# Two cross-attention layers on one core: the zeros of layer 0's transposed contexts set on GpSimd when their buffers are handed out

## The chip, the core and the metric

The kernel runs on one core of one Trainium2 chip. Its time is the device time of one execution in microseconds (us). The profile is one further execution, taken by the hardware profiler. Engines: PE (TensorE's matmuls; PEld its weight loads), DVE (VectorE), ACT (ScalarE), POOL (GpSimd), and SP (SyncE), which here only issues transfers; "SPq" rows are those issues. Every engine works through its own list of instructions in order; an instruction that waits holds up all behind it on that engine. SyncE's list is in order too: a transfer whose source or destination is not ready holds up the issue of all later ones.

## The reference

All data is float32. `x` is 8 batches of 100 rows of 512, `ctx_2048` 8 batches of 361 rows of 512.

```python
# layer 0, one head of 512
q = x @ w_q.T;  k = ctx @ w_k.T;  v = ctx @ w_v.T
probs = softmax(q @ k.T / sqrt(512))
x = x + alpha * ((probs @ v) @ w_o.T)
# layer 1: twice (1, 2) a cross-attention with 16 heads of 128, then an MLP
h = layer_norm(x)
kh = concat(ctx @ wk + bk, bias_k);  vh = concat(ctx @ wv + bv, bias_v)   # 361 + 1 keys
x = x + softmax((h @ wq + bq) @ kh.T / sqrt(128)) @ vh @ wo + bo
x = x + gelu(layer_norm(x) @ w_fc1 + b_fc1) @ w_fc2 + b_fc2
```

## The kernel before

Weights are multiplied together where that saves work: layer 0 needs only `wqk` and `wvo`, and in the layers after it the queries are multiplied with `wk` ("wide queries", `pqw`, L687), so that scores are taken against the raw context. For that every batch's context is needed transposed.

**The transposed contexts.** `ctx_transposed(b)` (L450) makes a tile `cT` of 128 partitions x 7 blocks x 2 x 181 numbers. The 361 keys are split in 181 and 180, so the second half has one padded key; the four blocks B11, B21, B22, T3 are what layer 0's scores read, T1, T2 and T4 are sums that later layers use. TensorE transposes (`pcT`, L457), ScalarE copies into B21, B22 and B11 (L460, L461, L463), VectorE subtracts into T3 (L464) and makes T2, T1, T4 (L466 to L468), which read whole blocks with the padded key. So the padded column must be zero: L452 sets it on VectorE, as the first instruction of the function. At the end the tile is stored to DRAM (`cTd`, L469, 1267 KB), from where the later layers load it again (L182).

**The ring.** `cT` tiles have two slots (`C_SLOTS`). A `Ring` (L23) keeps the planned order of uses; `issue()` makes a tile as soon as the ring's next slot is free of planned uses, and calls its `fill`:

```python
            key = self.order[self.next]
            name = "_".join(map(str, key))
            self.tiles[key] = self.pool.tile(self.shape, F32, tag=self.tag, name=name)
            self.fill(key, self.tiles[key])
```

For a later layer's `cT`, `fill_cT` (L180) issues the load from DRAM. For layer 0's (key[1] is -1) it does nothing, since the tile is written by compute. The pool gives out its slots in the order in which a scheduler meets the first instruction on each tile; what waits for the slot is that first instruction, and every other engine that writes the tile waits for the slot's last users as well.

**The order of layer 0** is written in `layer0_units` (L527). For each batch b: `l0_probs(b)` (transposes of the weights, `ppt` L348), `l0_scores(b + 1)` (`sc` L478, then L331 on VectorE and the exponential L334 on ScalarE), `l0_mixed(b)` (`pxc` L511, copied by ScalarE L514), `ctx_sums(b)`, `ctx_transposed(b + 2)`, the scaling (L341, L342) of b + 1, loads of the weights `wqe` (L156 on GpSimd's queue), `l0_out(b)` (`pd` L520, L521), which also stores the rows of x (`xd`, L376). `ctx_sums(b)` (L437) makes five sums of context blocks on GpSimd (L441 to L445) in one buffer (`msum`, bufs=1) and stores them to DRAM (`cxd`, L447, L448); the next batch's sums wait until both stores have landed. VectorE also multiplies the `wqe` weights (`bias_sums`, L603). In what follows, "cT 7" is layer 0's transposed context of batch 7.

**SyncE's queue** mixes all of this: at the end of layer 0 it issues, in this order, the store of cT 6 (L469), rows of x, a weight load, the load of layer 1's first cT (L182), the stores of batch 5's sums (L447, L448), the store of cT 7, rows of x, the stores of batch 6's sums with loads of layer 1's second context between them (L169 to L178, and a second L182), rows of x, a weight load, the stores of batch 7's sums, rows of x, then the bias scores of layer 1 (`sbd`, L647) and their return as one number per partition (`nsb`, L652, L653), and the weights of the heads, a pair at a time (`wkr`, `wq`, L156; `wkd`, L663).

**Layer 1's start.** `normed` (L566) takes the rows of x, `project_units` (L1132) makes transposed weights (`pwk`, L661), queries (`pq`, L671) and wide queries for two heads at a time. The first scores (`sc`, L478) go through L331, L334, L341 and L342 and are transposed on VectorE (L358). For the second block of queries the rows of x are loaded again (`xr`, L370) and normalised on VectorE (L579).

Of the kernel before, what the change touches and what calls it, by code (L numbers as in the profile page):

```python
# [38 lines left out]
KH = 181  # L39
B11, B21, B22, T1, T2, T3, T4 = range(7)  # L40
# [39 lines left out]
def two_cross_attentions(ctx: ExitStack, tc: tile.TileContext, a: dict, out: bass.AP):  # L80
    nc = tc.nc
# [10 lines left out]
    def psum(pool, shape, name):  # L92
        return pool.tile(shape, F32, tag=pool.name, name=name)
# [84 lines left out]
        nc.sync.dma_start(out=t[:TS, :, A33, :], in_=d[:TS, :, 0, :])  # L178

    def fill_cT(key, t):  # L180
        if key[1] >= 0:
            nc.sync.dma_start(out=t.rearrange("p u c s -> p (u c s)"), in_=cTd[key[2]])  # L182

    rings = {
        "ctx": Ring(cpool, [P, 20 * P], "ctx", C_SLOTS, fill_ctx),
        "ctx0": Ring(work, [P, 9 * GWIDTH // 2], "pT", 2, fill_ctx0),
        "cT": Ring(cpool, [P, 7, 2, KH], "cT", C_SLOTS, fill_cT),
        "w": Ring(wpool, [P, 1024], "w", W_SLOTS, fill_w),
        "v": Ring(vpool, [P, 1024], "v", V_SLOTS, fill_w),
# [243 lines left out]
    def ctx0(b):  # L433
        t = rings["ctx0" if b % 2 else "ctx"].tiles["ctx", -1, b]
        return t[:, : 3 * D].rearrange("p (k n) -> p k n", k=3)
# [13 lines left out]

    def ctx_transposed(b):  # L450
        ct, cx = rings["cT"].tiles["cT", -1, b], ctx0(b)
        tc.keep_in_program_order(nc.vector.memset(ct[:, B22 : T3 + 1 : T3 - B22, :, KH - 1 :], 0.0))  # L452
        for c in (2, 3, 0, 1):
            ps = psum(ps_mm, [P, S], f"pcT_{b}_{c}")
            for t in range(3):
                w = TS if t == 2 else P
                nc.tensor.transpose(ps[:, t * P : t * P + w], cx[:w, t, c * P : (c + 1) * P], ident[:w, :w])  # L457
            left, right, n = ps[:, :KH], ps[:, KH:], S - KH
            if c >= 2:
                nc.scalar.copy(ct[:, B21, c - 2, :], left)  # L460
                nc.scalar.copy(ct[:, B22, c - 2, :n], right)  # L461
            else:
                nc.scalar.copy(ct[:, B11, c, :], left)  # L463
                nc.vector.tensor_tensor(ct[:, T3, c, :n], right, ct[:, B22, c, :n], ALU.subtract)  # L464

        nc.vector.tensor_tensor(ct[:, T2], ct[:, B11], ct[:, T3], ALU.subtract)  # L466
        nc.vector.tensor_tensor(ct[:, T1], ct[:, B22], ct[:, T2], ALU.subtract)
        nc.vector.tensor_tensor(ct[:, T4], ct[:, B21], ct[:, T2], ALU.subtract)  # L468
        nc.sync.dma_start(out=cTd[b], in_=ct.rearrange("p u c s -> p (u c s)"))  # L469
# [57 lines left out]
    def layer0_units():  # L527
# [3 lines left out]
        def turned(b):  # L531
            return [unit(lambda: ctx_transposed(b), key0("ctx", b), key0("cT", b))] if b < B else []
# [844 lines left out]
```

## Time and profile before

| | us |
|---|---|
| runs (3) | 2013.85, 2010.42, 2009.63 |
| median | 2010.42 |
| the profiled execution | 2009.43 |
| its span, first to last instruction | 2007.7 |
| mean granted TensorE clock in it | 0.998 |
| PE, PEld busy | 1959.0, 1811.7 |
| DVE, ACT, POOL busy | 1277.3, 757.0, 707.6 |

The groups of the page that belong to the change, and the waits from 120 to 182 us in which the stretch after it shows:

```profile
engine line waited for: us in total, times, longest us
POOL rstd L382 <- DVE var L381: 16.8, 3, 9.2
...
ACT cT_-1_7_955 L460 <- DMA cTd<-cT_-1_6_853: 7.0, 1, 7.0
POOL p L325 <- DMA nsb<-sbd: 6.9, 1, 6.9
...
PE sc L478 <- ACT cT_-1_7_955 L463: 4.1, 1, 4.1
...
DVE xr L579 <- DMA xr<-xd: 1.5, 1, 1.5
```

Each row names the engine and line that stood still, what released it, the total, the number of times and the longest. A name such as `cT_-1_7_955` is ring key (layer -1, batch 7) and a buffer number. The eight L452 memsets take 62 ns each; they start at 48.1, 67.3, 72.1, 82.2, 96.9, 107.1, 115.0 and 133.0 us. In the chain of waits, the profile follows the end of the execution back, from each instruction to what released it; a share in it is time on the path that sets the end. The windows give, for stretches of the span, the busy time of each engine, the granted TensorE clock (1.00 is full) and the transfers.

### The profile page before, as it was taken

To read this page: it belongs to the slowest core of one execution; us is meant where nothing else is said; L and a number is where in the kernel's file an instruction comes from. 1 tells how busy PE (TensorE), PEld (TensorE's weight loads), DVE (VectorE), ACT (ScalarE), POOL (GpSimd) and SP (SyncE) were. 2 spreads that over 40 slices of the span, in tenths; PEclk is the share of its full clock that TensorE was granted. 3 is DMA by queue.
4 is the path that set the end of the run, shared out by engine and by line. 5 is a ranking of instruction groups with operands and counts; after the bars stand their busy time and mean duration, and the time that the engine had idled before them with its cause. 6 is when DMAs were issued, how large, how long until landed. Compare 5 with 4: busy or idle time off the path is not lost.

```text
span 2007.7 us, 31493 instructions
## 1 busy us (share of the span) xinstructions
PE 1959.0 (98%) x10991; PEld 1811.7 (90%) x10991; DVE 1277.3 (64%) x3523; ACT 757.0 (38%) x2002; POOL 707.6 (35%) x1147
## 2 busy tenths in 40 slices
PE   9989999999999999999999999999999999999999
PEld 5678899998999899999999999999999999889998
DVE  2554776667677677666775766676666667765543
ACT  1324544344442343344432444444433444421231
POOL 3233432543344144525243323333243243325140
PEclk9999999999999999999999999999999999999999
DMA  7686224742645356625534453235234432136442
GB/s 253 247 310 217 93 76 138 225 136 68 195 146 166 107 142 204 200 71 164 181 120 127 116 182 103 85 92 164 88 117 130 135 123 83 58 86 190 119 127 73
DMA packets 250682, 283.89 MB, mean 141 GB/s; under 512 B 37608, under 2 KB 212108, under 8 KB 247196
## 3 DMA queue, kind: packets, MB, share of 16 engines
q1 hardware_dynamic: 246340, 271.51, 43.4%
q0 software_dynamic: 2112, 6.40, 0.9%
q10 hardware_dynamic: 2072, 3.97, 0.6%
q8 instruction: 88, 1.44, 0.3%
q14 instruction: 70, 0.57, 0.1%
HBM read 242.86 MB, written 38.97 MB: 140 GB/s over the span
## 4 chain that ended last, share of the span: by engine, by line
PE 78%; DVE 12%; ACT 4%; DMA 2%; issue 2%; POOL 1%; SPq 0%; DVEq 0%; ACTq 0%; POOLq 0%
PE sx L731 9%; PE mx L841 9%; PE mz L841 7%; PE pq L671 7%; PE po L891 7%; PE pqw L687 7%; PE pwo_P L954 7%; DVE pT L358 6%; PE sz L731 5%; PE my L841 3%; PE sy L731 2%; PE pfx L1094 2%; PE sc L478 2%; PE pgx L1045 2%; ACT p L342 1%
## 5 line engine op out<-in xcount | busy, mean ns | idle before, releaser
L358 DVE STREAM_TRANSPOSE pT<-p 32x192 f32<-32x192 f32 (+1 forms) x1664 | 602.2, 362 | 84.2 <-ACT p L342 53.0
L841 PE MATMUL mx<-pT,ctx 128*128 128x256 f32 (+3 forms) x960 | 280.3, 391 | 9.6 <-DVE Z L867 4.0
L731 PE MATMUL sx<-cT,Z 128*128 128x181 f32 x1152 | 228.2, 317 | 2.2 <-DVE p L771 2.2
L841 PE MATMUL mz<-pT,ctx 105*128 105x256 f32 (+3 forms) x768 | 207.2, 391 | 9.4 <-POOL pT L805 6.6
L765 POOL TENSOR_SCALAR p<-nsb 128x1 f32<-128x1 f32 x192 | 38.9, 222 | 492.0 <-DVE pT L358 452.9
L731 PEld LDWEIGHTS sx<-cT,Z 128*128 128x128 f32 x1152 | 194.5, 190 | 14.7 <-DVE p L771 3.7
L841 PEld LDWEIGHTS mx<-pT,ctx 128*128 128x128 f32 (+1 forms) x960 | 169.8, 189 | 29.0 <-DVE Z L867 7.1
L687 PE MATMUL pqw<-q,wkT 128*128 128x200 f32 x1024 | 194.4, 332 | 0.0
L891 PE MATMUL po<-Z,wv 128*128 128x200 f32 x1024 | 192.7, 332 | 0.0
L671 PE MATMUL pq<-hT,wq 128*128 128x200 f32 x1024 | 192.3, 332 | 0.0
L785 ACT ACTIVATE p<-p,nm 128x362 f32<-128x362 f32 x192 | 114.8, 598 | 187.1 <-DVE nm L784 184.7
L841 PEld LDWEIGHTS mz<-pT,ctx 128*128 128x128 f32 (+1 forms) x768 | 143.7, 190 | 42.7 <-POOL pT L805 9.2
L687 PEld LDWEIGHTS pqw<-q,wkT 128*128 128x128 f32 x1024 | 176.2, 189 | 4.8
L891 PEld LDWEIGHTS po<-Z,wv 128*128 128x128 f32 x1024 | 175.2, 189 | 3.4
L671 PEld LDWEIGHTS pq<-hT,wq 128*128 128x128 f32 x1024 | 175.3, 189 | 3.0
L784 DVE TENSOR_REDUCE nm<-p 128x1 f32<-128x362 f32 x192 | 101.6, 529 | 104.1 <-ACT p L776 94.0
L690 ACT COPY Z<-pqw 128x400 f32<-128x400 f32 x256 | 123.0, 490 | 78.3 <-PE pqw L687 78.3
L731 PE MATMUL sz<-cT,sums 128*128 128x181 f32 x768 | 149.3, 316 | 0.7 <-ACT p L759 0.7
L714 POOL TENSOR_TENSOR sums<-Z 128x256 f32<-128x256 f32 x96 | 70.7, 736 | 223.4 <-ACT Z L690 134.8
L342 ACT ACTIVATE p<-p,rden 128x362 f32<-128x362 f32 (+2 forms) x216 | 129.1, 599 | 28.0 <-DVE rden L341 28.0
L731 PEld LDWEIGHTS sz<-cT,sums 128*128 128x128 f32 x768 | 124.8, 189 | 1.0 <-ACT p L759 1.0
L841 PE MATMUL my<-pT,ctx 128*128 128x256 f32 (+3 forms) x384 | 102.5, 388 | 0.0
(380 smaller groups left out, 3125.0 us busy)
## 6 DMA issues: line engine op xcount, KB each, us to landing
wv<-in_L_xattn_wv_dram SPq DMA_DIRECT2D x64, 512.0 KB
wq<-in_L_xattn_wq_dram SPq DMA_DIRECT2D x64, 512.0 KB
wkT<-wkd SPq DMA_DIRECT2D x48, 512.0 KB
cT<-cTd SPq DMA_DIRECT2D x16, 1267.0 KB
wo_S<-wod SPq DMA_DIRECT2D x32, 512.0 KB
f<-in_L_xattn_w_fc_dram SPq DMA_DIRECT2D x32, 512.0 KB
wo_A<-in_L_xattn_wo_dram SPq DMA_DIRECT2D x24, 512.0 KB
xr<-xd SPq DMA_DIRECT2D x45, 200.0 KB
```

The costliest lines, as they stand in the source:

```text
L342: nc.scalar.mul(p[:rows, :n], p[:rows, :n], rden[:rows])
L358: nc.vector.transpose(dst[keys, :, :, i, :], src[i * QD : (i + 1) * QD, :, :, quarter, :])
L671: nc.tensor.matmul(ps, w[:, c, (h % 2) * K : (h % 2 + 1) * K], hTs[l, q][:, c, :], start=(c == 0), stop=(c == DT - 1),)
L687: nc.tensor.matmul(ps[:, c, :], w[:, h % 2, cc * P : (cc + 1) * P], qs[h], start=True, stop=True)
L690: nc.scalar.copy(Z[:, 2 * c2 : 2 * c2 + 2, :, h * L : (h + 1) * L], ps.rearrange("p c (b t) -> p c b t", b=QB),)
L714: nc.gpsimd.tensor_tensor(t[:, 0], a2[:, :2, :], a2[:, 2:, :], ALU.add)
L731: nc.tensor.matmul(ps[:, :KH], st["a"][a][:, c, :], st["ct"][:, blk, c, :], start=(first and c == 0), stop=(c == 1), skip_group_check=not ...
L784: nc.vector.tensor_reduce(nm, p[:, :S1], AX.X, ALU.max, negate=True)
L785: nc.scalar.activation(p[:, :S1], p[:, :S1], AF.Exp, bias=nm, accum_out=den)
L841: nc.tensor.matmul(ps, cx[:w, blk, :], pT[:w, u, :], start=first, stop=last, skip_group_check=more)
L891: nc.tensor.matmul(ps, w[:, c, (h % 2) * K : (h % 2 + 1) * K], Z[:, c, :, h * L : (h + 1) * L], start=(c == 0), stop=(c == DT - 1),)
L954: nc.tensor.matmul(ps, w[:, h, :], OB[i, j][:, h, :], start=(h == 0 and not more), stop=(h == 7), skip_group_check=more)
```

## The change

The memset of the padded keys leaves `ctx_transposed`, where VectorE ran it in a fixed place of its order, and goes into `fill_cT`, on GpSimd, with no fixed place. `fill_cT` runs when the ring hands the tile out, which for batch b + 2 is right after the scores of batch b. So the tile's first instruction comes earlier in the program and is another engine's.

```diff
     def fill_cT(key, t):
-        if key[1] >= 0:
+        if key[1] < 0:
+
+            nc.gpsimd.memset(t[:, B22 : T3 + 1 : T3 - B22, :, KH - 1 :], 0.0)
+        else:
             nc.sync.dma_start(out=t.rearrange("p u c s -> p (u c s)"), in_=cTd[key[2]])
...
     def ctx_transposed(b):
         ct, cx = rings["cT"].tiles["cT", -1, b], ctx0(b)
-        tc.keep_in_program_order(nc.vector.memset(ct[:, B22 : T3 + 1 : T3 - B22, :, KH - 1 :], 0.0))
         for c in (2, 3, 0, 1):
```

What it does to the order of the built program, by comparing the two builds engine by engine:

- VectorE: eight memsets less. At the end of layer 0 the steps L464 to L468 of cT 7 now stand ahead of L521 of batch 5, the copy L319 and the statistics. At layer 1's start both L579 of `xr` now stand ahead of the first L331; before, one stood behind it and the other some ten instructions further on.
- GpSimd: eight memsets more. Those of batches 0 and 1 come right after the start's own; the one of batch b + 2 stands ahead of the sums of batch b, or right behind them for b = 0. The five loads of `wqe` 0 to 4, which stood ahead of or right behind the sums of batch 0, now stand behind the memset of cT 2.
- ScalarE: the exponential of batch 7 ahead of the copy L514 of batch 6, and one pair of copies at layer 1's start exchanged.
- TensorE: one of the transposes L423 moved behind scores of batch 0. SyncE: one `wkr` load ahead of a `wkd` store.
- Waits: the first write of cT 7 waited for the store of cT 6; now it waits for the store of cT 5. The load of layer 1's first cT (L182) had no wait for a cT store of its own; now it waits for the store of cT 6.

## The prediction

> **What bounds the kernel now.** I read the page's shares first, then the chain of waits in order of time, then the windows and the SyncE queue around the place that the change touches. The page's part 4 says where the end comes from:
>
> ```profile
> PE 78%; DVE 12%; ACT 4%; DMA 2%; issue 2%; POOL 1%; SPq 0%; DVEq 0%; ACTq 0%; POOLq 0%
> ```
>
> The kernel is TensorE's; only 2% of the chain are transfers. The change touches layer 0 alone, the first 155 of 2008 us, so it can only be worth what stands in that stretch. The chain in order of time has two transfers there:
>
> ```profile
> 123.67 0.47 DVE p L331 x2
> 124.16 0.55 ACT p L334
> 124.70 8.28 DMA cTd<-cT_-1_6_853
> 133.06 0.31 ACT cT_-1_7_955 L460
> ...
> 134.28 5.15 PE sc L478 x16
> 139.43 3.08 PE pxc L511 x24
> ...
> 171.00 1.37 PE pq L671 x8
> 172.55 1.19 SPq L156
> 173.79 7.15 DMA xr<-xd
> 181.15 0.34 issue
> 181.68 0.61 ACT p L342
> ```
>
> First: batch 7's transposed context cannot be written until batch 6's has been stored, 8.28 us after SyncE issued the store. Second: x rows fetched again for layer 1's second query block (xr). After it the chain runs over VectorE (normalise xr, L341, transposes L358) up to 208 us and only then back to TensorE. The windows (length, PE, PEld, DVE, ACT, POOL, granted clock, DMA share, GB/s) show what the first costs:
>
> ```profile
> 130.00:132.00 2.00, 0.22 (x3) 0.03 (x1) 0.00 (x0) 0.00 (x0) 0.00 (x0) 1.00 0.91 297
> 132.00:134.00 2.00, 0.00 (x0) 0.00 (x0) 0.98 (x3) 0.94 (x5) 0.00 (x0) 0.83 1.11 437
> 134.00:136.00 2.00, 1.72 (x6) 1.66 (x7) 1.88 (x7) 0.44 (x3) 0.00 (x0) 0.50 0.94 381
> 136.00:138.00 2.00, 2.00 (x8) 1.93 (x7) 2.00 (x14) 0.00 (x0) 0.55 (x1) 0.50 0.80 302
> 138.00:140.00 2.00, 2.00 (x9) 1.95 (x9) 1.20 (x10) 0.00 (x0) 0.54 (x1) 0.50 0.98 409
> ```
>
> TensorE stands still for 4.1 us and then runs at half clock for 6 us.
>
> **What the change removes there.** With two slots, batch 7 should follow batch 5. In the build before, the layer 1 load of cT (L182) took batch 5's slot, and batch 7 waits for batch 6's store. The listing of both builds with their waits shows the swap: in the changed build the L460 copy of batch 7 waits for the store of batch 5, and the L182 load for the store of batch 6. Batch 5's store was issued at 110.93 and the DMA share had fallen to 0.32 by 119 to 120, so it has landed. The copy can start when ACT is free, at 126.05 instead of 133.06, and the scores follow batch 6's transposes at 130.2 instead of 134.28. Locally: 4.1 us of wait; scores 5.15 against 2.46 us for every other batch, 2.7; mix 3.08 against 2.65, 0.4. Sum **7.2 us** by which TensorE ends layer 0 earlier.
>
> **Small parts.** Eight VectorE memsets of 0.062 us go, 0.5 us at most. Eight GpSimd memsets come: the nearest rows are 0.12 us for 128x1 and three of 128x46 in 0.29 us, so 0.1 us each. Each stands ahead of L441's sums of a later batch, which wait for the cxd store anyway (35.7 us in six waits). Memset b+2 waits for the store of cT b, which SyncE issues before that cxd store. Nothing, therefore; if that cover went, 0.1 us each. The memset of batch 2 also stands ahead of five weight loads (wqe, L156), which move from 18.9 to 26.1 to about 55, when batch 0's store (issued at 50.27, moved by 54) is in. DMA moves nothing from 54 to 65, the loads landed 6.0 to 14.6 us after issue, and L603 needs the first at 91: nothing. Freeing the queues around 20 us gives nothing either, since TensorE waits for no load between 4.4 and 65 us.
>
> **What it moves, and what is late next.** The wait does not vanish: L182 now has it, in the middle of SyncE's queue.
>
> ```profile
> 124.70 0.34 SPq L469 DMA_DIRECT2D cTd<-cT_-1_6_853  x1
> 125.17 0.31 SPq L376 DMA_DIRECT2D xd<-O  x1
> 125.58 0.65 SPq L156 DMA_DIRECT2D wkr<-in_L_xattn_wk_dram  x1
> 126.29 1.59 SPq L182 DMA_DIRECT2D cT<-cTd  x1
> 127.97 2.08 SPq L447 DMA_DIRECT2D cxd<-msum  x1
> ...
> 144.01 0.55 SPq L182 DMA_DIRECT2D cT<-cTd  x1
> 144.61 0.59 SPq L447 DMA_DIRECT2D cxd<-msum  x1
> ```
>
> Behind it are the cxd stores of batch 5, the store of cT 7, and all that follows. GpSimd's sums of batch 6 need those cxd stores (there is one buffer) and began at 139.46; then the cxd stores of batch 6, sums of batch 7 (152.19), cxd stores of batch 7 (155.67), then the bias scores (159.24), their return (nsb), and at 164.26 the weights wkr of the third pair of heads. This chain of stores and sums never saw TensorE's wait, so TensorE's 7.2 us do not shorten it. How it shifts:
> - The store of cT 6 lands at 133.0 with the L182 load beside it. Alone, the same 1267 KB of batch 0 were moved 3.7 us after issue, which here is 128.4. I take 131: the ctx loads issued up to 124.2 are still ahead of it, but no load is beside it.
> - From the L182 load to the landing of the cxd stores behind it: the second pair above took 144.01 to 152.19, 8.2 us, with little ahead. So 131.1 + 8.2 = 139.3 against 139.46: **-0.2 us** (ends: -2.8 from 128.4, +1.8 from 133.0).
> - The bias scores no longer wait 1.3 us for VectorE's sT, but share the queue with the cxd stores of batch 7: I take 0.8 (ends 0 and 1.3).
> So wkr, and the 4.2 MB of weights from there to xr that keep the DMA at 0.84 to 1.10 from 166 to 180 us, come **1.0 us** earlier (ends: 4.1 earlier, 1.8 later). TensorE, 7.2 us early, reaches the third pair's transposes (L661) at 162.8 instead of 169.96 and waits: with wkr issued near 163.3 and, as before, at most 5.7 us to landing, until about 168.5. The gain is spent there, and xr lands at 180.0 instead of 181.03.
>
> Then VectorE's order counts. Before, the first layer 1 score (L331) ran at 178.91, ahead of xr's normalisation (L579, 181.03), and L341 followed at 181.49. In the changed build both L579 of xr stand ahead of L331. So after xr: two L579 (0.46 + 0.45, the second row set landing some 0.2 later), then L331 and the exponential, 1.6 us from L331 to L341's earliest start in the rows (0.53, 0.6, 0.19 and gaps): L341 at 180.0 + 2.5 = 182.5, 1.0 later. At 185.02 the second L579 is no longer in the way, -0.5. **Sum: +0.5 us** (ends -2.6 and +3.3) on a path that the chain shows to be the last up to 208 us. From there all engines' orders are the same, and the shift is carried to the end.
>
> TensorE's idle stretch of about 5.7 us will cost it its clock again. Rows: after 4.1 us of idle it had half clock from 134.3 to about 140.2; at the start 0.85 us instead of 0.43 a matmul up to 10.4. Six us at half clock cost 3 us; the first scores of layer 1 then end at 178.7 - 1.5 + 3.0 = 180.2, and L331 cannot start before 181.0 anyway: hidden, with 0.8 us to spare.
>
> The Trainium skill, TensorE: Matmul & The Clock Gate (Part 1), puts the half-rate stretch at about 3.4 us of sustained work, which would make that price 1.7 us; this trace has 6 us, and the trace decides. The Trainium skill, DMA: Bandwidth & Descriptors (Anatomy of one DMA), fits 2.0 us + bytes / 436e3; for 1267 KB that is an estimate of 5.0 us, a landing at 129.7 and a sum of -0.8 instead of +0.5; the 8.28 us of the trace, in a full queue, speak against it.
>
> **Rivals.**
> 1. The gain survives: 7.2 us less, 2002.7. For it: the two transfers on the chain are apart by 40 us, TensorE is 98% busy, and what TensorE has gained it would keep if xr came with it. Against: the cxd chain above, whose next start (139.46) stands on a DMA, not on TensorE. It would need the third pair's weights some 6 us earlier; no row moves them by more than 4.1.
> 2. Slower: the wait that L182 takes over. Everything behind it in SyncE's queue starts when the store of cT 6 lands, and the net is +0.5 at a landing of 131 with 0.8 from the bias scores. If those give nothing and it lands at 135, the net is 4.0 + 1.3 = +5.3, 2015.2. It exceeds 4 us from a landing of 133.7, just past the 133.0 of now; L182 alone is not on the queue to delay it, which speaks against.
> 3. It does not do what it says: batch 7 still waits, because its memset stands in GpSimd's queue behind other waits. Then the time stays as it is. Against: GpSimd is free at 119.6, 6 us ahead of the copy.
>
> **How the numbers follow.** The profiled execution took 2009.43 us (span 2007.7 and 1.7 around it); the median of the runs, 2010.42, lies 1.0 above it, the lowest 0.2 above. 2009.43 + 0.5, and 0.5 for a median's usual place: **2010.4**. About 0.2%, 4 us, is what a measurement of this kernel can tell from no change. Chances: the forecast 0.74, rival 3 with the same time 0.06, rival 1 (wholly or by over 4 us) 0.11, rival 2 0.09. So faster 0.11, same 0.80, slower 0.09. The range goes from 2009.43 - 2.6 to 2009.43 + 3.3 + 1.0, rounded outwards: 2006.5 to 2014.0.
>
> **What would show it.** Right: scores of batch 7 at about 130 us at full clock with no wait for a cT store; L182 on SyncE waiting until about 131; cxd of batch 7 still issued at about 155 to 156; a TensorE wait of 4 us or more for wkr near 163 with the clock low after it; xr landing near 180 and both L579 ahead of L331. Wrong: sums of batch 6 well before 137, no wait at the third pair's transposes, or xr landing before 177; then rival 1 wins. A landing of cT 6 after 133.7 makes it rival 2.

## The result, and the profile after

The changed kernel takes 2016.93 us (median of 8 runs, 2015.07 to 2020.16), the kernel before 2010.92 us (median of 8 runs): a ratio of 1.003, 95% interval 1.002 to 1.004. So it is about 6 us slower, and the interval lies clear of 1. The forecast was 2010.4 us with a range of 2006.5 to 2014.0, and "within 0.2%" at 0.80. It was wrong, on the side of rival 2.

The profiled execution took 2016.93 us, its span 2014.7. Below, lines up to 454 of the kernel before are +3 in the changed kernel and later ones +2. First the shares of the chain of waits after the change:

```profile
PE 78%; DVE 10%; DMA 4%; ACT 4%; issue 2%; POOL 1%; SPq 0%; DVEq 0%; ACTq 0%; POOLq 0%
```

Transfers have gone from 2% to 4%, VectorE from 12% to 10%. The wait that left ScalarE is now SyncE's, between 110 and 180 us, with a second one further on that comes up below:

```profile
SPq L156 <- DMA wkd<-wkT: 8.0, 2, 5.2
SPq L185 <- DMA cTd<-cT_-1_6_854: 6.8, 1, 6.8
```

(engine and line, what released it; us in total, times, longest). The chain in order of time (start us, length us, what) shows which transfers:

```profile
123.56 8.43 DMA cTd<-cT_-1_6_854
132.06 0.34 SPq L185
132.50 0.58 SPq L450
133.14 7.48 DMA cxd<-msum
140.78 0.73 POOL msum L444
...
146.06 7.41 DMA cxd<-msum
153.59 0.73 POOL msum L444
...
159.33 2.90 DMA sbd<-sT
162.24 0.55 SPq L654
...
164.91 0.65 SPq L156
165.61 6.67 DMA wq<-in_L_xattn_wq_dram
172.41 5.67 PE pq L673 x16
178.08 2.94 PE pqw L689 x16
181.03 2.46 PE sc L480 x16
```

Before, the chain left the store of cT 6 for TensorE's scores of batch 7. Now those scores run at 129.2 at full clock, and the chain stays with the transfers: store of cT 6, the load L185 that waits for it in SyncE's queue, cxd stores of batch 5, sums of batch 6, cxd stores of batch 6, sums of batch 7, bias scores (sbd, nsb), weights. TensorE, 8 us earlier than before at 154, stands still for the weights:

```profile
PE pwk L663 <- DMA wkr<-in_L_xattn_wk_dram: 4.1, 1, 4.1
PE pq L673 <- DMA wq<-in_L_xattn_wq_dram: 4.0, 2, 2.3
```

(in the same form). The first 2.3 us of the second row are the second pair's `wq`, before 159.06. What follows these waits, in windows (PE busy is the second number; the granted clock is the third from the right):

```profile
164.00:166.00 2.00, 0.74 (x5) 0.43 (x3) 0.00 (x0) 0.99 (x2) 0.31 (x2) 1.00 0.53 4
166.00:168.00 2.00, 0.00 (x0) 0.00 (x0) 0.00 (x0) 0.00 (x0) 2.00 (x8) 1.00 1.09 237
168.00:170.00 2.00, 1.21 (x6) 1.21 (x7) 0.00 (x0) 0.00 (x0) 2.00 (x4) 0.55 0.82 153
170.00:172.00 2.00, 0.76 (x4) 0.36 (x2) 0.69 (x1) 0.59 (x1) 0.08 (x1) 0.50 1.03 391
...
176.00:178.00 2.00, 2.00 (x8) 2.00 (x7) 0.00 (x0) 0.00 (x0) 0.00 (x0) 0.50 0.92 329
178.00:180.00 2.00, 2.00 (x12) 2.00 (x11) 0.00 (x0) 1.22 (x3) 0.00 (x0) 0.89 0.96 350
```

TensorE is at half clock from 168.2 to 178.4. It reaches layer 1's first scores at 180.9; before, at 176.25. VectorE is no earlier:

```profile
182.44 0.55 DVE L581 TENSOR_SCALAR xr<-xr,mv,rstd 100x512 f32<-100x512 f32 x1 [11.75 <-DMA xr<-xd]
183.40 0.55 DVE L581 TENSOR_SCALAR xr<-xr,mv,rstd 100x512 f32<-100x512 f32 x1 [0.41 <-DMA xr<-xd]
183.86 0.58 DVE L334 TENSOR_SCALAR_CACHE_REDUCE p<-sc,nsb 64x361 f32<-64x361 f32 x1
```

Both paths end within 0.4 us: the scores at 183.49, the second normalisation of `xr` at 183.86, when the row maximum (L334) starts. To see where the time goes in every run, I matched TensorE's instructions of each trace with those of before and noted how many us later (+) each comes, at five places of before's time:

| kernel | 60 | 154 | 173.5 | 195 | 300 | median - before |
|---|---|---|---|---|---|---|
| changed | -1.1 | -8.0 | +4.3 | +3.7 | +3.7 | +6.0 |
| e1 | -0.2 | +0.8 | +0.8 | +3.4 | +3.4 | +3.3 |
| e2 | -0.4 | -7.0 | +1.3 | +2.3 | +2.3 | +3.2 |
| e3 | 0.0 | -3.3 | -2.8 | -1.2 | -1.2 | +0.5 |
| e4 | +0.1 | +0.1 | +0.1 | +0.7 | +0.7 | +1.9 |
| e5 | -0.8 | -0.6 | -0.6 | -1.3 | -1.3 | +0.4 |
| e6 | -1.0 | -7.1 | -0.7 | -1.4 | -1.4 | +1.4 |
| e7 | -1.0 | -4.4 | +3.2 | +4.3 | +4.3 | +7.0 |
| e8 | -0.7 | -4.0 | +3.6 | +9.4 | +9.4 | +10.9 |
| e9 | +0.1 | -6.8 | -6.8 | -2.7 | -2.7 | +1.4 |
| e10 | +0.5 | -2.4 | -2.4 | -1.5 | -1.5 | -1.9 |
| e11 | -0.1 | -7.9 | -7.9 | -3.9 | -3.9 | -3.9 |
| e12 | -0.7 | -6.6 | -5.8 | -6.5 | -6.5 | -4.7 |
| e13 | -1.3 | -9.1 | -9.1 | -10.0 | -8.6 | -6.1 |
| e14 | -0.4 | -4.2 | +3.2 | +2.4 | +3.8 | +6.8 |
| e15 | 0.0 | -3.4 | +0.4 | -0.5 | +1.0 | +4.8 |
| e16 | -0.5 | -7.3 | -7.3 | -8.2 | -6.6 | -4.0 |

The first column is the start's scatter, not the change. The loss of the changed kernel lies between 154 and 195 us. From 300 us to the end every run loses 0.5 to 4.5 us more against before's profile, e3 too (3.6), whose order there is before's; I take the changed kernel's 3.3 there to be of that kind: before's one profiled execution, 1.5 us below its median, would then be a lucky one in that part. So the two traces place 3.7 us in this stretch; where the rest of the 6 us by the medians arises they do not settle. The medians decide.

**The gain in layer 0 differs from execution to execution.** The changed kernel, e6, e7, e8, e14 and e15 have one and the same order of every engine in layer 0, yet TensorE ends layer 0 at 146.5, 147.4, 150.1, 150.5, 150.3 and 151.2 us. Before's profile has 154.5; e3 and e10, whose tiles are claimed in before's order, have 151.2 and 152.2, and TensorE does not wait for batch 7's context in either. In e3:

```profile
114.54 0.81 DVE L603 SCALAR_TENSOR_TENSOR wqe<-wqe,Z 128x128 f32<-128x128 f32 x1
117.69 3.68 PE L520 MATMUL pd<-Z,xc 128*100 128x512 f32 x8 [1.43 <-ACT xc L514]
129.80 3.68 PE L520 MATMUL pd<-Z,xc 128*100 128x512 f32 x8 [1.81 <-ACT xc L514]
133.58 2.30 PE L478 MATMUL sc<-cT_-1_7_955,Z 128*100 128x181 f32 x12
```

VectorE's sums of `wqe` ran beside GpSimd's sums there (0.81 us instead of 0.28 for one; more on this with e1), TensorE waited 3.2 us for xc in two waits, and by then the store of cT 6 had almost landed: ScalarE's copy waited 0.9 us for it. In before's profile the two engines just missed each other, by 0.7 us at batch 4 (VectorE ends at 114.6, GpSimd begins at 115.31) and by 0.2 us at batch 5 (123.66, 123.88). So the wait of 4.1 us and the half clock behind it are those of an execution in which they miss. Where they meet, layer 0 ends at 150.1 to 151.2 with the early claim and at 151.2 and 152.2 without: some 1 us.

### The profile page after: what moved, and what is told of

Read it like the earlier page. It is cut to its first block, busy times and chain, and to the rows that moved or that the text cites. A ratio compares the mean times of both kernels' runs of the same rounds, so it can differ in the third digit from the quotient of the medians.

```text
span 2014.7 us, 31524 instructions
## 1 busy us (share of the span) xinstructions
PE 1961.0 (97%) x10991; PEld 1813.5 (90%) x10991; DVE 1280.3 (64%) x3515; ACT 756.6 (38%) x2002; POOL 708.5 (35%) x1155
## 4 chain that ended last, share of the span: by engine, by line
PE 78%; DVE 10%; DMA 4%; ACT 4%; issue 2%; POOL 1%; SPq 0%; DVEq 0%; ACTq 0%; POOLq 0%
PE sx L733 10%; PE mx L843 9%; PE mz L843 7%; PE pq L673 7%; PE pwo_P L956 7%; PE po L893 7%; PE pqw L689 7%; DVE pT L361 5%; PE sz L733 5%; PE my L843 3%; PE sy L733 2%; PE pfx L1096 2%; PE sc L480 2%; PE pgx L1047 2%; ACT p L345 1%
```

## The experiments

Theory A at the start: the wait that has moved into SyncE's queue delays all that stands behind it. Rivals: B, the transfers and the half clock take any gain of TensorE there; C, the zeros on GpSimd, or the weight loads held behind them, cost it.

**e1 and e2: the load out of the queue's way.** Same edit on the changed kernel (e1) and on the kernel before (e2).

```diff
+        elif key[1:] in ((0, 0), (0, 1)):
+            kept_cT[key[2]] = t            # loaded later by late_cT(b)
...
             res.append(unit(lambda b=b: ctx_sums(b), key0("ctx", b)))
+            if b >= 6:
+                res.append(unit(lambda b=b: late_cT(b - 6)))
```

> The changed kernel, with the first two layer 1 loads of cT issued later: that of batch 0 behind the cxd stores of batch 6, that of batch 1 behind those of batch 7, so that no load that waits for a store of a transposed context stands ahead of cxd stores in SyncE's queue. Theory A (the wait that moved into SyncE's queue delays the cxd stores, the sums, the bias scores and so the weights of the third pair): cxd of batch 5 issued near 127 instead of 132.5, third pair's wkr before 159 instead of 164.9, no TensorE wait over 1.5 us between 155 and 180, and the 5 to 7 us that TensorE gained at batch 7 stay: 2003 (2001 to 2006). Theory B (what TensorE gains is lost to the weights or to the half clock whatever SyncE's queue does): 2009 or more. Theory C (the zeros on GpSimd or the four weight loads held behind them are the loss): as the changed kernel, 2015 to 2018.

> The kernel before, with the same two loads issued later and nothing else: the zeros stay on VectorE, at the place where they were. With the load of batch 0 out of the way, batch 7's transposed context is the first to claim batch 5's place, as in the changed kernel. Theory A: the order of claims is all that the change brings, so the time is that of e1 within 2 us, 2003 (2001 to 2006). Theory C (GpSimd's part costs something): e1 is slower than this one by over 2 us. Theory B: 2009 or more in both.

Measured: e1 2014.26 us, 1.002 (1.0008 to 1.0032) of before; e2 2014.15, 1.002 (1.001 to 1.003). The two are equal, and 2.7 us below the changed kernel by the medians, but not at 2003: A alone doesn't hold. That they are equal speaks against C only weakly, since the traces show two different losses. In e2 TensorE keeps its 7 us up to 154, and then the chain reads

```profile
144.04 3.68 PE pd L527 x8
...
152.27 8.05 DMA sbd<-sT
160.34 0.55 SPq L661
...
163.01 0.66 SPq L156
163.72 6.65 DMA wq<-in_L_xattn_wq_dram
```

The bias scores go to memory at 152.27, 7 us earlier than in the changed kernel, but land after 8.05 us instead of 2.90, since my deferred 1267 KB load of batch 1's cT was issued at 148.69, right ahead of them (in e5 below, without that load ahead, 1.4 us). SyncE waits for them, and the weights' loads stand behind (L156). So I took the bias scores' trip for the gate, not the cxd stores as such; e6 tests it.

In e1 TensorE has lost its gain by 146, in layer 0 itself. VectorE's sums of `wqe`:

```profile
135.68 0.28 DVE L614 SCALAR_TENSOR_TENSOR wqe<-wqe,Z 128x128 f32<-128x128 f32 x1
...
135.90 2.49 DVE L614 SCALAR_TENSOR_TENSOR wqe<-wqe,Z 128x128 f32<-128x128 f32 x1
...
138.32 0.86 DVE L614 SCALAR_TENSOR_TENSOR wqe<-wqe,Z 128x128 f32<-128x128 f32 x1
```

and GpSimd's row, in the same trace:

```profile
136.16 0.72 POOL L451 TENSOR_TENSOR msum<-ctx_-1_6_768 128x256 f32<-128x256 f32 x1
```

The same instruction takes 0.28 us until GpSimd's sums of batch 6 begin at 136.16; the one that runs then takes 2.49, the next two 0.86 and 0.80. The row maximum of batch 7 waits behind them, ScalarE's copy of xc behind that, TensorE stands 3.40 us, and its clock is halved from 142.9 to 146.3. It had lost some 3 us at batches 4 and 5 in the same way. That the late load brought this on isn't shown: e10 has one of 2.28 us at the same place without it. The Trainium skill, SBUF — State Buffer (Who interferes with whom), states that a VectorE instruction with two SBUF inputs contends with a GpSimd instruction that reads SBUF, and calls the shared ports an exclusive lock; 0.80 beside 0.28 fits a wait for one GpSimd instruction of 0.72 to 0.83, the 2.49 is longer than one.

**e3: the engine alone.**

```diff
-        tc.keep_in_program_order(nc.vector.memset(ct[...], 0.0))
+        tc.keep_in_program_order(nc.gpsimd.memset(ct[...], 0.0))
```

> The kernel before, with the engine of the zeros changed alone: GpSimd sets them, pinned at the place where VectorE did, and the claims stay as they were. Theory A: no difference, 2010.5 (2009 to 2012.5), the wait of the batch 7 copy for the store of batch 6 still there. Theory C: slower by 2 us or more.

Measured: 2011.42, 1.0001 (0.9991 to 1.001): no difference. So GpSimd's zeros cost nothing that can be measured. The wait for batch 6's store, expected to stay, was 0.9 us of ScalarE's and none of TensorE's, for the reason given above. The weight loads held behind the zeros have no run of their own; e13 below has both and is no slower than e16, which has neither. With that rival C falls.

**e4: the sums cut loose from the stores.**

```diff
+        if b % 2:
+            t = zf[:, 10240:11520].rearrange("p (m u n) -> p m u n", m=2, n=P)
+        else:
             t = work.tile([P, 2, 5, P], F32, tag="pb", name=f"msum_{b}", bufs=1)
```

> The changed kernel, with a second buffer for GpSimd's sums (odd batches put theirs where the product of layer 0's output weights has been read for good). The load of batch 0 still waits some 7 us in SyncE's queue, but the sums of a batch no longer wait for the cxd stores of the batch before. Theory A: the loss comes through that chain, so wkr of the third pair is issued before 160 and the time is 2006 (2003 to 2010). Theory B or C: no gain against the changed kernel, 2014 or more.

Measured: 2012.8, 1.0007 (0.9994 to 1.002): 4.1 us of the 6 come back; L185 still waits until 132.78. The time lies between the two forecasts, above A's 2010 and below 2014. wkr went out at 163.61, not before 160, and in the profiled execution TensorE had lost its gain in layer 0 already (+0.1 at 154), so that it met the weights without a wait and kept its clock there.

**e5 and e6: the bias scores' trip.** e5 moves the load of batch 1's cT far behind; e6 leaves all loads as the change has them and puts the trip in GpSimd's queue.

```diff
+            if n == 0 and j == 0:          # e5: in the middle of layer 1's first step, pinned
+                fill[at] = both_of(unit(lambda: late_cT(1)), fill[at])
...
-                nc.sync.dma_start(out=nsb[:, j, 1:], in_=...)
+                nc.gpsimd.dma_start(out=nsb[:, j, 1:], in_=...)    # e6: and sbd, first query block
```

> As e1 (the changed kernel, cT of batch 0 loaded for layer 1 behind the cxd stores of batch 6), but the load of batch 1's cT is pinned far behind, after the weights of the third to fifth pair and xr, so that no 1267 KB load stands right ahead of the bias scores. Theory A2 (the gain is lost in SyncE's queue, where the weights stand behind the bias scores' trip to memory and back, and that trip is long when a cT transfer or cxd stores are ahead of it: 8.05 us in e2): the trip takes about 3 us, wkr of the third pair is issued by 160, TensorE waits for it under 1.5 us, and the time is 2006 (2003 to 2010). Theory B (DMA throughput around 160 to 180 or VectorE's order sets it, whatever stands ahead of the bias scores): as e1, 2014 (2011 to 2017).

> The changed kernel, with the bias scores' trip of the first query block (sbd stores, nsb loads) issued from GpSimd's queue instead of SyncE's; the load of cT stays where the change has put it. SyncE then no longer waits for sbd, and the weights of the third pair follow the store of wkT. Theory A2: wkr issued near 160.5 instead of 164.9, its wait on TensorE (4.1 us) gone to under 1 us, half clock gone with it, first score of layer 1 at 176 or earlier: 2011 (2008 to 2013). Theory A alone (the cxd chain, which is unchanged here, sets it): 2015 to 2018. GpSimd's issue may cost a little more than SyncE's.

Measured: e5 2011.07, 0.9998 (0.9984 to 1.0013); e6 2012.04, 1.0013 (1.0004 to 1.0023). Against the changed kernel 5.9 and 4.9 us less; e6 lies in its range, e5 1 us above A2's and at the lower end of B's. In e6 wkr was issued at 159.44, and TensorE reached the first scores at 175.6, as forecast; its waits and one step of half clock did not go altogether. TensorE's waits between 150 and 180 in e6:

```profile
PE pq L674 <- DMA wq<-in_L_xattn_wq_dram: 2.4, 2, 1.3
PE pwk L664 <- DMA wkr<-in_L_xattn_wk_dram: 1.6, 1, 1.6
```

8.1 us have become 4.0. So on the changed kernel 4.9 of the 6 us hang on the weights' place behind a trip that SyncE waits for. (The same edit on the kernel before, e10 below, gains 1.9 us; with the trip moved in both, the change still costs 3.3.) In e5 TensorE had lost 3 us to VectorE's sums, as in e1 (one took 2.29 us).

**e7 and e8: the half clock.** 34 matmuls of the identity ahead of the third pair's transposes; in e7 `xr` is pinned where it was, in e8 it goes ahead of the fifth pair's wkr.

```diff
+        if (l, p) == (0, 2):
+            idle = psum(ps_t, [P, D], "idle")
+            for i in range(34):
+                tc.keep_in_program_order(nc.tensor.matmul(idle[:, :P], ident, ident, start=True, stop=True))
```

> The changed kernel, with 34 matmuls of the identity (results unused) ahead of the third pair's transposes, about 4 us at 0.12 us each, where TensorE waits for wkr; the loads of xr are pinned behind the fifth pair's wq, where they are in the changed kernel. Theory H (the half clock that the wait brings on is what makes the change slower): the transposes take 1.04 instead of 1.97, the queries 2.9 instead of 5.7, and the time falls by 3 to 4 us to 2013. Theory X (VectorE's path over xr, landed at 182.44, is late by itself and would end at most 0.4 us sooner): full clock as said, yet 2016.5 (2014.5 to 2018.5).

> As e7 with nothing pinned: the loads of xr then go out ahead of the fifth pair's wkr, behind the fourth pair's wq, some 5 us earlier. Theory X, both paths being equally late in the changed kernel: with both relieved, about 3 us less than the changed kernel, 2013.5 (2011.5 to 2015.5), and less than e7. Theory H: no further gain against e7.

Measured: e7 2017.62, 1.0035 (1.0023 to 1.0047); e8 2021.53, 1.0056 (1.0041 to 1.0071). Each matmul ran as two, 7.75 us in all, twice what I had meant; even so TensorE had full clock and reached the first scores at 179.43 instead of 180.86. It gained nothing; `xr` came at 182.97: theory X, as forecast. e8 is a miss. There VectorE took the normalisation of `xr` ahead of the copy of wkT (L323), TensorE waited 4.1 us for that copy, and the run tells nothing of H against X, only that `xr` in VectorE's order holds back what stands behind it.

**e9 and e10: both cures; and the trip alone, on the kernel before.** e9 is the edits of e5 and e6 on the changed kernel, e10 that of e6 on the kernel before.

> Both cures on the changed kernel: the bias scores' trip in GpSimd's queue (e6) and the two cT loads moved behind (e5). Theory A2 (SyncE's queue alone holds the gain back): no wait of TensorE over 1 us from 150 to 180, first score of layer 1 near 170, and 2005 (2003 to 2008). Theory P (VectorE's sums of wqe, which take 0.29 us each alone and 0.73 to 2.5 us beside GpSimd's sums, eat the gain when the cxd stores come earlier, as in e1 and e5, where TensorE had lost 3 us by batch 7's mix): 2009 (2007 to 2012).

> The kernel before, with only the bias scores' trip moved into GpSimd's queue. TensorE waits for no weights there, and the first score of layer 1 stays at 176; only xr can come earlier, by up to 3 us, of which VectorE can use 1.5: 2010 (2008 to 2012). If it gains 4 us or more, the trip in SyncE's queue was a bound of the kernel before as well, and the change is not what brought it on.

Measured: e9 2012.29, 1.0007 (0.9997 to 1.0018); e10 2008.99, 0.999 (0.998 to 0.9999). In e9 no wait for weights is left, and TensorE reaches layer 1's first scores at 169.42, the 6.8 us in hand. Then `xr`: the second row set could be normalised only at 175.23, that stands ahead of the row maximum on VectorE, and TensorE waited 3.15 us for a buffer and had half clock after it. Both A2 and P were off; the next gate was one of theory X. e10 gains 1.9 us, within its bounds: the trip was a small bound before (1.9 us), and a larger one with the change (4.9).

**e11 and e12: VectorE's sums of wqe behind the row maximum.** On e9's kernel, and on e10's.

```diff
-            res += scored(b + 1)
+            res += scored(b + 1) + waiting    # the sums of wqe of the iteration before
+            waiting = []
...
-                res += summed(p)
+                waiting += summed(p)
```

> As e9, and VectorE's sums of wqe are emitted behind the exponential's row sums (L334) of the following batch instead of ahead of them, so that they no longer stand between TensorE's scores and the mix. Theory P: the 3 us come back, TensorE reaches layer 1's first score at 170 or earlier, and the time is 2004 (2001 to 2007), below e9 by 3 us or more. Theory A2 alone: as e9.

> The kernel before, with the bias scores' trip in GpSimd's queue and the sums of wqe behind, but the claims as they were (batch 7 waits for batch 6's store). What e11 gains over this one is what the early claim is worth once nothing behind it takes the gain back: by theory A2 with P 5 us, this one at 2009 (2007 to 2011). If the two are equal, TensorE's wait at batch 7 is worth nothing in any of these orders.

Measured: e11 2007.04, 0.9981 (0.9971 to 0.9991); e12 2006.23, 0.9981 (0.9969 to 0.9994). e11 is 5 us below e9 by the medians, at the upper end of P's range (2007), but 1.2 us by the traces at 195: in e9's profiled execution VectorE's sums happened to miss GpSimd's, and P rests on the medians alone. The gate at `xr` is still there (VectorE's and TensorE's waits between 160 and 180 in e11):

```profile
DVE xr L593 <- DMA xr<-xd: 10.5, 2, 5.4
```

```profile
PE sz L746 <- ACT p L774: 3.0, 1, 3.0
```

e12 came out 2.8 us below its forecast and is as fast as e11 without the early claim. Two things differ. In e12 the store of cT 6 goes out at 121.96 instead of before's 124.70, TensorE waits only 1.7 us for batch 7's context and is 6.6 us early at 154, so that the claim had little left to take. And before's order has the row maximum (L331, at 173.14) ahead of the first normalisation of `xr` (174.43): the gate at `xr` comes with the change, and e11 loses 4 us there.

**e13 to e16: the last gate, the clock, and the claim's own worth.** The one new edit pins the normalisation of `xr` at its place in the program, far behind; e13 has it on e11, e14 on the changed kernel alone, e15 on e14 with half as many matmuls of the identity as e7 and, as there, `xr`'s loads pinned, e16 on e12.

```diff
-                nc.vector.tensor_scalar(h, h, mv[:, b, 0:1], ...)
+                ins = nc.vector.tensor_scalar(h, h, mv[:, b, 0:1], ...)
+                if (n, q) == (0, 1):
+                    tc.keep_in_program_order(ins)
```

> As e11, and the normalisation of the second query block's rows (xr) is pinned at its place in the program, far behind the first row maximum of layer 1, instead of ahead of it. Theory X (VectorE waits for xr in front of work that TensorE needs: 5.4 us in e11): the 3 us wait of TensorE for sz's buffer and the half clock behind it go, about 4 us, 2003 (2000.5 to 2005.5). Rival: another wait takes its place (weights of the fourth or fifth pair, sums on GpSimd), as e11, 2007.

> The changed kernel with that one pin alone. TensorE's own first score ended at 183.65, VectorE's row maximum began at 183.86, so there is 0.2 us to be had: 2016.7 (2014.5 to 2018.5). If xr alone held the changed kernel back, 2013 or less.

> As e14, with 17 matmuls of the identity (34 passes, about 3.9 us; results unused) ahead of the third pair's transposes, and xr's loads pinned where they are in the changed kernel. With xr out of VectorE's way, what is left of the difference to e14 is the price of the half clock: transposes 1.04 instead of 1.97, queries 2.9 instead of 5.7, in sum 3 us: 2013.7 (2011.5 to 2016). If equal to e14, the half clock costs nothing and the loads alone set it.

> The kernel before, with the bias scores' trip in GpSimd's queue, the sums of wqe behind the row sums and the same pin (e12 and the pin), the claims as before. The wait of batch 7 for the store of batch 6 was only 1.7 us in e12, so the early claim with the late loads (e13) should be 1.7 us faster or less: this one at 2005.5 (2003 to 2008).

Measured: e13 2004.66, 0.9972 (0.9961 to 0.9983); e14 2017.5, 1.0028 (1.0018 to 1.0038); e15 2015.51, 1.0025 (1.0015 to 1.0034); e16 2006.76, 0.9982 (0.9972 to 0.9991). All four went as forecast within their bounds. e13's chain, from batch 7's scores to layer 1, has no transfer:

```profile
128.23 2.46 PE sc L488 x16
130.70 2.67 PE pxc L521 x24
133.93 3.68 PE pd L530 x8
...
164.57 2.71 PE pqw L704 x16
167.28 2.46 PE sc L488 x16
169.74 0.61 PE sx L748 x4
```

e14 shows that `xr` alone was not the bound; e15 against e14 puts the half clock's price at about 2 us by the medians (2.9 at 195 us by the traces) once `xr` is out of the way, but the two intervals overlap, so that this price isn't shown. e13, 6.1 us faster than before and 12 faster than the changed kernel, keeps the whole local gain. The pin has a small price: TensorE waits 1.8 us for the late normalisation between 195 and 300 us, in e13 and e16 alike. e13 is the version to use; the share of the early claim and the late loads in it is 2.1 us (e16 against e13; 1.7 or less was forecast), which the two overlapping intervals do not show to be more than nothing. With VectorE's sums out of the way, TensorE's wait at batch 7 is 0.8 us in e16, where it was 4.1 in before's profile, so little is left for the claim to take.

## Why the prediction was wrong

None of the signs of being wrong that the prediction named appeared; it failed on a path that it had called hidden.

- **The local gain: right for the two traces, and in part luck.** 7.2 us were forecast; TensorE ends layer 0 8.0 us earlier, of which 1.1 are the start's scatter. Scores of batch 7 at 129.2 at full clock, no wait for a cT store. But the wait was read from one execution: in e3 and e10 TensorE has none at that place with the claims as before, and in four of the six executions of the changed layer 0 the gain is smaller (see the result).
- **The wait moves to L182 (now L185): right in place.** It waits 6.8 us, and all named behind it are late.
- **The store of cT 6 lands at 131: wrong.** It took 8.43 us against 8.28 before, although no load was beside it; I had given it 6.3. It landed at 132.06, and the trace is 1.1 us ahead of before's from the start, so 2.2 us worse than I had it. (That lies within the end of 133.0 that I had allowed it, but for 0.2 us.) Ahead of it in the queue stood the cxd stores and ctx loads issued from 117.50 to 122.13; no run took them away, so that they are the reason is argued, not shown.
- **8.2 us from there to the cxd stores' landing: 8.7.** So sums of batch 6 at 140.78 instead of 139.3.
- **Bias scores 0.8 us earlier: 0.** They no longer waited for VectorE's sT (1.3 us before), but their stores, close behind cxd stores, took 2.90 instead of 1.6; the cxd stores of batch 7 went out at 157.09, not at 155 to 156. So wkr was issued at 164.91, not 163.3: 0.65 us later than before, not 1.0 earlier. These three are the terms of one sum, which came to +0.65 in the trace's own time, +1.8 with the start taken out; that is the end of the range that I had given (+1.8).
- **TensorE waits from 162.8 to 168.5: 164.7 to 168.8.** Right in its end; it came to that place 1.9 us later, since it had waited 2.33 us for the second pair's wq, which I had not looked for.
- **"Hidden, with 0.8 us to spare": the step that failed most.** I had the half clock last 6 us and the first scores end at 180.2. It lasted 10.2 us, through another wait for weights (the third pair's wq, 1.65 us) that I had not looked for either, and the scores ended at 183.49. To TensorE's path I had added the price of one wait, wkr's; but the third pair's wq lands late too, at 172.3, 6.67 us behind its issue.
- **xr at 180.0: 182.44.** Besides the weights' 1.8 us, SyncE took the fifth pair's wkr ahead of a wkd store, waited 5.2 us there for an earlier wkd store, and issued xr at 175.09 instead of 173.79. The order was in the listing and named in the change's section; I gave it no price. e14 shows that this path alone was not the bound: with the pin, and no other edit, the time is 2017.5.
- **Both L581 ahead of L334, +1.0 - 0.5:** the order was right, and from xr to L344 it took 2.8 us where I had 2.5, but on an xr that was 2.4 us later.
- **Rival 2** had the right side and mechanism (what stands behind L182 starts late) and a price that was near (+5.3 for +6.0), but the wrong condition: cT 6 landed before 133.7, at 132.06 (133.2 with the start taken out). The decision fell behind it, at the bias scores' trip and at the clock.
- **Rival 1's condition**, third pair's weights some 6 us earlier, is what e13 fulfils (wkr issued at 149.74 instead of 164.26), and there the gain is kept. The range should have gone beyond +3.3: I had bounded each transfer, but not two paths late together.

Not settled: how often VectorE's and GpSimd's sums meet in layer 0 of each kernel, and so how much of e1's and e5's loss there is their order and how much chance. e11 and e13, in which VectorE's sums stand elsewhere, do not lose time to it.

## What to carry to other kernels

When a wait is taken from an engine, follow what it was hiding: here four gates stood one behind another (a load in front of stores in one queue, a memory round trip in front of weights, sums of two engines that block each other, a normalisation in front of a row maximum), and the gain was whole only when all were open. Most of it (4.0 of 6.1 us) then comes without the change. A wait put in an in-order queue is paid by what stands behind it. Look at a second execution before you call a wait the kernel's: whether the 4.1 us were there hung on 0.2 to 0.7 us between two other engines. Ask of every stall that a fix creates whether the clock falls with it, and how many stalls follow within the next few us.

## What the runs showed of the hardware

The half clock comes in whole steps. By windows of 0.2 us, the granted clock was at 0.50 from 133.3 to 140.1 in the kernel before, 168.2 to 178.4 in the changed one, 168.5 to 172.0 in e6, 169.9 to 176.7 in e14 and 142.9 to 146.3 in e1: 6.8, 10.2, 3.4, 6.8 and 3.4 us, that is 2, 3, 1, 2 and 1 steps of 3.4 us. In these five it rose only behind a step in which TensorE was busy throughout: in the changed kernel the step from 171.6 to 175.0, in which it worked 2.6 us, from 172.41 on, did not lift it. In e2 a step with 3.2 us of work was enough. In e6 it fell without any wait over 1.6 us, behind a step (165.1 to 168.5) in which TensorE worked about 1.2 us. The Trainium skill, TensorE: Matmul & The Clock Gate (Part 1), has a free-running window of 3.4 us; the prediction read it as a rival of the 6 us in the trace, and the two agree: 6.8 us are two such windows.

The other is VectorE beside GpSimd, shown with e1: 0.28 us alone, 0.80 to 0.87 beside in most cases, and one each of 2.49, 2.29 and 2.28 (e1, e5, e10).
